# Autocorrelation of a two-layer decoder: the shifted sums as two products of 64 rows over mirrored tokens

## Chip, cores and metric

The kernel runs on one core of a Trainium2 chip. The metric is the device time of one execution in microseconds (us). The core has five engines with queues of their own: PE (TensorE, matrix products and transposes), DVE (VectorE), ACT (ScalarE), POOL (GpSimd) and SP (SyncE, which here only issues transfers). An engine takes its instructions in order; an instruction that waits holds up what is queued behind it on that engine.

## The reference, cut to what matters

A decoder of two layers over 8 samples of 128 tokens and 512 channels: block attention, autocorrelation with a context, and a mixture of experts in layer 0; attention over 256 tokens, cross attention and a second mixture in layer 1. The change is in the autocorrelation. In it Q is the sequence, K and V are both the context:

```
qf = jnp.fft.fft(q, axis=2)
kf = jnp.fft.fft(k, axis=2)
corr = jnp.fft.ifft(qf * jnp.conj(kf), axis=2).real
topk = int(C * np.log(L))                       # 9
w, idx = jax.lax.top_k(corr.transpose(0, 1, 3, 2), topk)
w = jax.nn.softmax(w, axis=-1)
pos = jnp.arange(L)[:, None]
for i in range(topk):
    g = jnp.minimum(idx[:, :, None, :, i] + pos, L - 1)
    out = out + w[:, :, None, :, i] * jnp.take_along_axis(v, g, axis=2)
```

Each channel picks nine shifts, and sums its context shifted by them, weighted; a shift past the last token reads the last token.

## The kernel before

A tile has the 128 tokens of a sample in the partitions and 512 channels along the row (or, after a transposition, 128 channels in the partitions and 4 x 128 tokens). All is float32; the profile shows every product of float32 as two passes on PE. The autocorrelation is done with matrices of cosines and sines, which lie in the table `dft` (its columns at T_A, T_I, T_W, T_V, T_J).

Samples go in four pairs, each an object of `Correlated`, in these steps:

- `spectra`: the waves of the sequence (pa) and of the context (pb), 64 frequencies each (L398); the two samples of a pair lie in the lower and upper 64 partitions. ACT copies pa out (xa), DVE multiplies (pr, L408 and L410), POOL adds and subtracts (L409, L411).
- `correlate`: the inverse transform, products of 64 rows (pc, L420), copied out by ACT (co, L425).
- `chosen(h)` for each sample: the nine largest shifts by MAX8 and match_replace on DVE (L435 to L441, into wk1, a tile of one buffer), exp of the differences (POOL L443, ACT L444), the mask (DVE L445), sum and reciprocal (L447, L449), and the normalized weights ex (POOL L450).
- `shifted(h)`: ex transposed (pt_wT, L129; copied out as wT), the waves of the context over 255 tokens (pvf, L460) and of the weights (pw, L464), each as two products of 128 rows, cosine and sine; ACT copies pw out twice (wf, L469 and L470), so that DVE can take it in the other order; DVE multiplies (vw, L472 and L474), POOL adds and subtracts (L473, L475).
- `done(h)`: back to tokens (poc), residual and layer norm (DVE L103, L91 to L95, POOL L97 for the root, DVE L107).

The context of a pair is loaded by `context(p)` (L314) into two buffers, tag "ct". For pairs 0 and 1 the steps stand as `pieces` in the loop of layer 0's attention (L516 to L547), two places a round: between its exps, its value products and its projections. `spectra` and `correlate` of pair 2 come behind that loop (L550 to L560); the rest of pair 2 and pair 3 stands in the mixture of experts, whose steps R (routing), E (experts) and T (tokens turned) are interleaved by hand with `chosen`, `shifted` and `done` (L731 to L768). In the following, samples are numbered 0 to 7, two to a pair. The order on every engine follows from the order of the calls, but for places under `issue_after`, which hold an instruction back behind a named one, and from which buffers are free.

Of the kernel before, what the change touches and what calls it, by code (L numbers as in the profile page):

```python
# [11 lines left out]
F32 = mybir.dt.float32  # L12
AF = mybir.ActivationFunctionType
ALU = mybir.AluOpType
# [3 lines left out]
P = 128  # L18
B, S, D = 8, 128, 512
NC = D // P  # L20
# [10 lines left out]

C_CAUSAL, C_HEAD = 0, 3 * P
C_SIGN = 3 * P + 2
N_MASK = 3 * P + 3
T_A, T_I, T_W, T_V, T_J = 0, P, 3 * P, 5 * P, 7 * P
N_DFT = 9 * P


def bc(ap, shape):
# [4 lines left out]
def decoder(ctx: ExitStack, tc: tile.TileContext, a: dict, out: bass.AP):  # L44
# [34 lines left out]
    causal = masks[:, C_CAUSAL : C_CAUSAL + 3 * P]  # L79
    pair = masks[:, C_HEAD : C_HEAD + 2]  # L80
    sign = masks[:, C_SIGN : C_SIGN + 1]

    def mm_acc(ps, pairs):
        n = len(pairs)
# [296 lines left out]
    def swapped(t):  # L381

        return t[:, 1:3, :]

    class Correlated:
# [5 lines left out]
        def spectra(self):  # L391

            ps = {}
            for n, src in (("a", xs), ("b", cts)):
                ps[n] = banks(f"p{n}_{self.p}")
                for i in range(2):
                    for h, b in enumerate(self.bs):
                        nc.tensor.matmul(  # L398
                            ps[n][64 * h : 64 * h + 64, i, :],
                            lhsT=dft[:, T_A + 64 * i : T_A + 64 * i + 64], rhs=src[b], start=True, stop=True,  # L400
                        )
                if n == "a":
                    xa = cp.tile([P, 3, D], F32, tag="sp", name=f"xa_{self.p}", bufs=2)
                    nc.scalar.copy(xa[:, 0:2, :], ps[n])

                    nc.scalar.mul(xa[:, 2, :], ps[n][:, 0, :], sign)
            self.pr = [cp.tile([P, 2, D], F32, tag="prod", name=f"pr_{self.p}_{i}", bufs=3) for i in range(2)]
            nc.vector.tensor_tensor(self.pr[0], ps["b"], xa[:, 0:2, :], ALU.mult)  # L408
            nc.gpsimd.tensor_tensor(self.pr[0][:, 0, :], self.pr[0][:, 0, :], self.pr[0][:, 1, :], ALU.add)  # L409
            nc.vector.tensor_tensor(self.pr[1], ps["b"], swapped(xa), ALU.mult)  # L410
            nc.gpsimd.tensor_tensor(self.pr[1][:, 0, :], self.pr[1][:, 0, :], self.pr[1][:, 1, :], ALU.subtract)  # L411

        def correlate(self):
            pc = banks(f"pc_{self.p}")
            for i in range(NC):
                cols = slice(i * P, (i + 1) * P)
                for n in range(2):
                    for h in range(2):
                        rows = slice(64 * h, 64 * h + 64)
                        nc.tensor.matmul(  # L420
                            pc[:, h, cols], lhsT=self.pr[n][rows, 0, cols],
                            rhs=dft[rows, T_I + n * P : T_I + (n + 1) * P], start=(n == 0), stop=(n == 1),
                        )
            self.co = cp.tile([P, 2, NC, P], F32, tag="co", name=f"co_{self.p}")
            nc.scalar.copy(self.co.rearrange("p h c t -> p h (c t)"), pc)  # L425

        def chosen(self, h):

            b, co = self.bs[h], self.co[:, h]

            top = sm.tile([P, NC, 8], F32, tag="top", name=f"top_{b}")
            nxt = sm.tile([P, NC, 8], F32, tag="nxt", name=f"nxt_{b}")
            wk1 = cp.tile([P, NC, P], F32, tag="wk1", name=f"wk1_{b}")
            for i in range(NC):
                nc.vector.max(top[:, i, :], co[:, i, :])  # L435
                nc.vector.match_replace(wk1[:, i, :], top[:, i, :], co[:, i, :], BIG)
                nc.vector.max(nxt[:, i, :], wk1[:, i, :])

            nc.vector.memset(nxt[:, :, TOPK - 8 :], BIG)
            for i in range(NC):  # L440
                nc.vector.match_replace(wk1[:, i, :], nxt[:, i, :], wk1[:, i, :], BIG)  # L441
            ex = cp.tile([P, NC, P], F32, tag="ex", name=f"ex_{b}", bufs=2)
            nc.gpsimd.tensor_tensor(ex, co, bc(top[:, :, 0:1], [P, NC, P]), ALU.subtract)  # L443
            nc.scalar.activation(ex, ex, AF.Exp)  # L444
            nc.vector.scalar_tensor_tensor(ex, wk1, BIG, ex, ALU.is_equal, ALU.mult)  # L445
            su = sm.tile([P, NC], F32, tag="su", name=f"su_{b}")
            nc.vector.tensor_reduce(su, ex, AX.X, ALU.add)  # L447
            rc = sm.tile([P, NC], F32, tag="rcw", name=f"rcw_{b}")
            nc.vector.reciprocal(rc, su)  # L449
            nc.gpsimd.tensor_tensor(ex, ex, bc(rc.unsqueeze(2), [P, NC, P]), ALU.mult)  # L450
            self.ex[h] = ex

        def shifted(self, h):
            b = self.bs[h]
            wT = cp.tile([P, NC, P], F32, tag="wT", name=f"wT_{b}")
            transposed(self.ex[h].rearrange("p c t -> p (c t)"), NC, P, wT, f"wT_{b}", "a")
            pv = banks(f"pvf_{b}")
            pw = banks(f"pw_{b}")
            for i in range(2):
                nc.tensor.matmul(  # L460
                    pv[:, i, :], lhsT=dft[:, T_V + i * P : T_V + (i + 1) * P], rhs=cts[b], start=True, stop=True
                )
            for i in range(2):
                nc.tensor.matmul(  # L464
                    pw[:, i, :], lhsT=dft[:, T_W + i * P : T_W + (i + 1) * P],
                    rhs=wT.rearrange("p c t -> p (c t)"), start=True, stop=True,
                )
            wf = cp.tile([P, 3, D], F32, tag="sp", name=f"wf_{b}", bufs=2)
            nc.scalar.copy(wf[:, 0:2, :], pw)  # L469
            nc.scalar.copy(wf[:, 2, :], pw[:, 0, :])  # L470
            vw = [cp.tile([P, 2, D], F32, tag="prod", name=f"vw_{b}_{i}", bufs=3) for i in range(2)]
            nc.vector.tensor_tensor(vw[0], pv, wf[:, 0:2, :], ALU.mult)  # L472
            nc.gpsimd.tensor_tensor(vw[0][:, 0, :], vw[0][:, 0, :], vw[0][:, 1, :], ALU.add)  # L473
            nc.vector.tensor_tensor(vw[1], pv, swapped(wf), ALU.mult)  # L474
            nc.gpsimd.tensor_tensor(vw[1][:, 0, :], vw[1][:, 1, :], vw[1][:, 0, :], ALU.subtract)  # L475
            self.ri[h] = [t[:, 0, :] for t in vw]

# [38 lines left out]
    for n, (p, f) in enumerate(steps):  # L516
        if f == 0:
            oTs.append(ap.tile([P, 2, NC, P], F32, tag="oT", name=f"oT0_{p}"))
        qT, kbd = qk
        units = []  # L520
        for j in range(2):
            toks = slice(j * P, (j + 1) * P)
            of = lambda i, w, p=p, f=f, j=j: vs[p, j][i].rearrange("p a x d -> p (a x d)")[:, f * w : (f + 1) * w]
            units.append((qT[:, toks], kbd[:, :, toks], lambda of=of: of(0, 192), lambda of=of: of(1, 128)))
        now = Heads16(ap, units, causal_bias, oTs[p][:, :, f, :], f"a0_{p}_{f}")
        now.exps(0)
        catch_up(now.scored)

        if turned:
            turned.out()  # L530
        if n + 1 < len(steps):
            qk = queries_keys(*steps[n + 1])
        if prev:
            prev.turn()
        auto(n, 0)

        for made in values_at.get(n, ()):
            values(*made)
        now.exps(1)
        if 0 < f < 3 and p:  # L540
            projection(2 * p - 3 + f, oTs[p - 1])
        if f == 1 and p and p + 1 < NP:
            xts.append(tokens(p + 1))
        auto(n, 1)
        if n >= begun and f == NC - 1:
            context(n // NC)
        turned, prev = prev, now  # L547
    assert not beside
# [4 lines left out]
    transposed(xs[1], NC, P, fp_tokens[1], "xTf0_1", "a")  # L553
    prev.turn()
    autos_of[2].spectra()
    prev.out()
    for j in range(2):
        projection(B - 2 + j, oTs[NP - 1])
# [184 lines left out]
    R(2)  # L743
    third.shifted(1)
    fourth.spectra()
    E(1)
    T(3)
    third.done(1)
# [519 lines left out]
def _mask_table():  # L1268
# [3 lines left out]
    t[:, C_CAUSAL : C_CAUSAL + 3 * P] = np.concatenate([half, half])  # L1272
    t[:, C_HEAD : C_HEAD + 2] = (np.arange(P)[:, None] // HD) % 2 == np.arange(2)
    t[:, C_SIGN] = np.where(np.arange(P) % 64 == 0, -1.0, 1.0)
    return t


# [11 lines left out]
def _dft_table():  # L1289
# [15 lines left out]
    for n, part in enumerate((cos, sin)):  # L1305
        t[:, T_I + n * P :][:, :P] = np.concatenate([2 * part / S] * 2)

    n = 2 * S - 1
    cos, sin = waves(n, np.arange(n), s)
    t[:, T_W : T_W + P], t[:, T_W + P : T_W + 2 * P] = cos[:S], sin[:S]  # L1310
    for i, whole in enumerate((cos, sin)):

        t[: S - 1, T_V + i * P :][:, :P] = whole[: S - 1]
        t[S - 1, T_V + i * P :][:P] = whole[S - 1 :].sum(0)
    c = np.where(s == 0, 1.0, 2.0)[:, None] / n
    cos, sin = waves(n, s, s)
    t[:, T_J : T_J + P], t[:, T_J + P : T_J + 2 * P] = c * cos, c * sin
    return t.astype(np.float32)


# [6 lines left out]
def _layouts(i):  # L1327
# [9 lines left out]
        "x": x,  # L1337
        "xT": xT,
        "ctx": c,
        "ctxT": cT,  # L1340
        "masks": _mask_table(),
        "dft": _dft_table(),
# [55 lines left out]
```

## Time and profile before

| | |
|---|---|
| three runs | 880.20, 883.38, 884.53 us, median 883.38 |
| profiled execution | 883.9 us; its span 882.1 us, so 1.8 us lie around the span |
| mean granted clock of PE | 0.994 |
| DVE, ACT, POOL busy | 62%, 42%, 21% of the span |
| transfers | 50.73 MB, 58 GB/s over the span |

On PE, from pa to the last poc, pair 0 lies at 85 to 146 us, pair 1 at 145 to 203, pair 2 at 208 to 259, pair 3 at 250 to 312. The transposed weights (pt_wT) and the products behind them come at 112 and 129 us for samples 0 and 1, at 174 and 191 for samples 2 and 3, at 231 and 245 for 4 and 5, at 274 and 292 for 6 and 7. A row of the timeline gives the start and the length of a run of like instructions in us, the engine, the line, the operation, the tiles (out<-in), the shapes, and in brackets how long the engine had been idle and what ended that. A row of the waits gives the engine and the line that waited, what for, the total in us, how often, and the longest. "Pass" below is one MATMUL record.

### The profile page before, as it was taken

To read this page: it belongs to the slowest core of one execution; us is meant where nothing else is said; L and a number is where in the kernel's file an instruction comes from. 1 tells how busy PE (TensorE), PEld (TensorE's weight loads), DVE (VectorE), ACT (ScalarE), POOL (GpSimd) and SP (SyncE) were. 2 spreads that over 40 slices of the span, in tenths; PEclk is the share of its full clock that TensorE was granted. 3 is DMA by queue.
4 is the path that set the end of the run, shared out by engine and by line. 5 is a ranking of instruction groups with operands and counts; after the bars stand their busy time and mean duration, and the time that the engine had idled before them with its cause. 6 is when DMAs were issued, how large, how long until landed. Compare 5 with 4: busy or idle time off the path is not lost.

```text
span 882.1 us, 17898 instructions
## 1 busy us (share of the span) xinstructions
PE 853.1 (97%) x6482; PEld 529.9 (60%) x6482; DVE 545.8 (62%) x2166; ACT 369.3 (42%) x1535; POOL 188.5 (21%) x267
## 2 busy tenths in 40 slices
PE   9999999999899999999999999999999999999996
PEld 5766655655455455555555687758475846576454
DVE  3656787777869567777778622735363545467654
ACT  3877564754222136666666503213122322224310
POOL 2500223133333314555555300000000000000000
PEclk9999999999999999999999999999999999999999
DMA  8700000130300002000004010331213211313340
GB/s 327 306 2 26 1 14 13 49 108 1 144 13 24 1 1 97 2 1 2 2 2 145 27 72 1 75 88 42 48 37 85 44 47 37 83 43 76 81 97 36
DMA packets 30073, 50.73 MB, mean 58 GB/s; under 512 B 5536, under 2 KB 22048, under 8 KB 28192
## 3 DMA queue, kind: packets, MB, share of 16 engines
q1 hardware_dynamic: 27424, 47.49, 17.9%
q10 hardware_dynamic: 2560, 2.10, 1.1%
q8 instruction: 51, 0.84, 0.4%
q14 instruction: 38, 0.31, 0.1%
HBM read 30.69 MB, written 2.10 MB: 37 GB/s over the span
## 4 chain that ended last, share of the span: by engine, by line
PE 72%; DVE 17%; ACT 6%; POOL 2%; issue 1%; DMA 1%; SPq 0%; ACTq 0%; POOLq 0%; DVEq 0%
PE pqx L86 9%; PE pox L994 7%; PE pv L86 5%; PE pkx L86 4%; PE pvx L86 4%; PE s_x L932 4%; PE o_x L977 4%; PE pq L86 4%; PE pk L86 3%; PE po L711 3%; ACT e_a L197 3%; DVE e_a L184 3%; PE pt_a L228 3%; PE pof L618 2%; PE s_a L165 2%; PE po L86 2%
## 5 line engine op out<-in xcount | busy, mean ns | idle before, releaser
L197 ACT ACTIVATE e_a<-e_a,m_a 128x128 f32<-128x128 f32 (+1 forms) x512 | 184.8, 365 | 100.2 <-DVE m_a L184 100.2
L953 ACT ACTIVATE e_x<-s_x,m_x 128x256 f32<-128x256 f32 x128 | 58.6, 483 | 140.0 <-DVE m_x L943 132.1
L197 ACT ACTIVATION_READ_ACCUMULATOR e_a<-e_a,m_a 128x1 f32 x512 | 97.6, 191 | 0.0
L86 PE MATMUL pqx<-xTx,w_X_q 128*128 128x256 f32 x384 | 84.9, 380 | 0.0
L86 PEld LDWEIGHTS pqx<-xTx,w_X_q 128*128 128x128 f32 x384 | 72.6, 190 | 11.4 <-issue 1.8
L994 PE MATMUL pox<-w_X_o,oTx 128*128 128x512 f32 x168 | 74.1, 596 | 0.7 <-DVE oTx L983 0.6
L942 DVE TENSOR_REDUCE m_x<-s_x 128x4 f32<-128x1024 f32 x32 | 37.6, 1218 | 41.2 <-PE s_x L932 41.2
L97 POOL TENSOR_TENSOR rs_x<-ve_x,neghalf 128x1 f32<-128x1 f32 x7 | 3.8, 548 | 268.8 <-DVE ve_x L95 249.8
L211 POOL TENSOR_TENSOR e_a<-e_a,rc_a 128x512 f32<-128x512 f32 (+1 forms) x64 | 52.7, 845 | 34.9 <-DVE rc_a L208 19.3
L994 PEld LDWEIGHTS pox<-w_X_o,oTx 128*128 128x128 f32 x168 | 31.3, 190 | 40.9 <-issue 39.2
L932 PE MATMUL s_x<-kTx,qTx 32*128 32x256 f32 x768 | 50.0, 385 | 1.2 <-ACT e_x L953 1.1
L228 PE MATMUL pt_a<-ident,e_a 128*128 128x128 f32 x384 | 48.0, 273 | 2.7 <-DVE m_a L184 2.7
L228 PEld LDWEIGHTS pt_a<-ident,e_a 128*128 128x128 f32 x384 | 43.6, 140 | 11.1 <-issue 5.0
L184 DVE CUSTOM_DVE_ANT_0 e_a<-s_a,masks 128x128 f32<-128x128 f32 (+1 forms) x256 | 47.1, 252 | 4.5 <-PE s_a L165 3.2
L932 PEld LDWEIGHTS s_x<-kTx,qTx 32*128 32x128 f32 x768 | 39.0, 184 | 17.4 <-issue 11.7
L184 DVE CUSTOM_DVE_ANT_0 e_a<-s_a,alibi 128x128 f32<-128x128 f32 (+1 forms) x256 | 47.4, 253 | 2.2 <-PE s_a L165 1.3
L977 PE MATMUL o_x<-pT_x,vx 128*32 128x512 f32 x384 | 43.7, 595 | 1.9 <-issue 0.7
L184 DVE DVE_READ_ACCUMULATOR2_ANT m_a<- 128x1 f32 x512 | 42.4, 83 | 0.1
L961 DVE STREAM_TRANSPOSE e_x<-e_x 128x1024 f32<-128x1024 f32 x32 | 39.7, 1241 | 0.8
L960 DVE TENSOR_SCALAR e_x<-e_x,rc_x 128x256 f32<-128x256 f32 x128 | 36.3, 347 | 3.9 <-DVE rc_x L957 2.2
L165 PEld LDWEIGHTS s_a<-kbd,qT 32*64 32x64 f32 x1024 | 20.7, 131 | 28.5 <-issue 15.4
L103 DVE TENSOR_TENSOR x_x<-pox,x_a 128x512 f32<-128x512 f32 x7 | 4.8, 686 | 52.5 <-PE pox L994 52.5
(236 smaller groups left out, 1627.1 us busy)
## 6 DMA issues: line engine op xcount, KB each, us to landing
pT_x<-e_x SPq DMA_DIRECT2D x224, 64.0 KB, 2.0
w_X_q<-in_X_q SPq DMA_DIRECT2D x3, 1024.0 KB, 4.8
w_X_o<-in_X_o SPq DMA_DIRECT2D x3, 1024.0 KB, 4.7
w_L_Wv<-in_L_Wv SPq DMA_DIRECT2D x2, 1024.0 KB, 7.3
w_L_Wo<-in_L_Wo SPq DMA_DIRECT2D x2, 1024.0 KB, 8.0
x_in<-in_x SPq DMA_DIRECT2D x8, 256.0 KB, 8.5
ct<-in_ctx SPq DMA_DIRECT2D x8, 256.0 KB, 2.6
cT<-in_ctxT SPq DMA_DIRECT2D x4, 512.0 KB, 3.8
```

The lines of the kernel that those rows point to most:

```text
L86: nc.tensor.matmul(ps, lhsT=l, rhs=r, start=(i == 0), stop=(i == n - 1))
L165: nc.tensor.matmul(s[r // 2][64 * u : 64 * u + 64, r % 2, cols], lhsT=qT[rows, 64 - 64 * part : P - 64 * part], rhs=kbd[rows, :, :keys], s ...
L184: self.scored = nc.vector.tensor_tensor_reduce(self.e[:, r, cols], s[i][:, r % 2, cols], bias(r, cols), -1.0, 3e38, ALU.add, ALU.min, self ...
L197: nc.scalar.activation(e[:, r, x, :], e[:, r, x, :], AF.Exp, scale=-1.0, bias=self.m[:, part, r, x : x + 1], accum_out=self.su[:, part, r, ...
L211: nc.gpsimd.tensor_tensor(e, e, bc(self.rc[:, part, rs, :].unsqueeze(3), list(e.shape)), ALU.mult)
L228: nc.tensor.transpose(pt[:, r, cols], self.e[:, 2 * i + r, cols], ident)
L932: nc.tensor.matmul(sc[g // 2][:, g % 2, u * 256 : (u + 1) * 256], lhsT=qT[rows, (h0 + u) * NS + n, :], rhs=kT[rows, n], start=(n == 0), st ...
L942: nc.vector.tensor_reduce(m, self.s[i], AX.X, ALU.max, negate=True)
L953: nc.scalar.activation(self.e[:, :, j, :], self.s[half][:, i, :].rearrange("p (a k) -> p a k", k=32), AF.Exp, bias=self.m[:, j : j + 1], s ...
L961: nc.vector.transpose(self.e[:, :, js, :], self.e[:, :, js, :])
L977: nc.tensor.matmul(po[32 * g : 32 * g + 32, :], lhsT=v[:, s, g * XD + 32 * n : g * XD + 32 * n + 32], rhs=pT[:, s].rearrange("p i h x -> p ...
L994: nc.tensor.matmul(po, lhsT=oT[:, n, h * P : (h + 1) * P], rhs=w, start=(i == 0), stop=(i == NX - 1))
```

## The change

Context and weights are split into sums and differences of mirrored tokens, so that cosine needs only the sums and sine only the differences: 64 rows each. The tables T_W and T_V shrink from 256 to 128 columns (cosine in rows 0 to 63, sine in rows 64 to 127), the table `dft` from 1152 to 896. What is new per pair and per sample:

- `spectra` also issues two transfers of 256 KB for each sample, the context in a mirrored order (`ctx_down`) and another order (`ctx_up`); the second takes a buffer of tag "ct".
- `folded`, called at the end of `correlate`: per sample one DVE scalar_tensor_tensor that makes sums and differences, held back behind `Correlated.behind` (the last MAX of the step's scores in the loop, the variance of the last layer norm in the later part), one transfer of the last token's row to 64 partitions, and two POOL subtracts on 64 partitions.
- `chosen`: two more POOL operations of 128x256 that add and subtract the weights' halves, one read backwards; they write into wk1, which is then what `shifted` transposes.
- `shifted`: pvf and pw are each two products of 64 rows, in the upper and the lower half of the rows; the second ACT copy (L470) goes, since DVE reads wf backwards.
- xa has one buffer instead of two; wf has a tag of its own, with one buffer.
- the call context(3) moves from the last round of the loop behind `spectra` of pair 2.

```diff
             nc.gpsimd.tensor_tensor(self.pr[1][:, 0, :], self.pr[1][:, 0, :], self.pr[1][:, 1, :], ALU.subtract)
+            self.folds = [cp.tile([P, D], F32, tag="ct", name=f"fold_{b}", bufs=2) for b in self.bs]
+            self.down = [cp.tile([P, D], F32, tag="down", name=f"down_{b}", bufs=2) for b in self.bs]
+            for b, f, down in zip(self.bs, self.folds, self.down):
+                nc.sync.dma_start(down, a["ctx_down"][b])
+                nc.sync.dma_start(f, a["ctx_up"][b])
+
+        def folded(self):
+            for b, f, down in zip(self.bs, self.folds, self.down):
+                with tc.issue_after(Correlated.behind.ins):
+                    nc.vector.scalar_tensor_tensor(f, down, fold, f, ALU.mult, ALU.add)
+                end = cp.tile([P, D], F32, tag="down", name=f"end_{b}", bufs=2)
+                nc.sync.dma_start(end[:64, :], a["ctx"][b, S - 1].partition_broadcast(64))
+                for _ in range(2):
+                    nc.gpsimd.tensor_tensor(f[:64, :], f[:64, :], end[:64, :], ALU.subtract)
+                cts[b] = f
...
             nc.scalar.copy(self.co.rearrange("p h c t -> p h (c t)"), pc)
+            self.folded()
...
             nc.gpsimd.tensor_tensor(ex, ex, bc(rc.unsqueeze(2), [P, NC, P]), ALU.mult)
-            self.ex[h] = ex
+            up, down = ex[:, :, 64:], ex[:, :, 63::-1]
+            for i, op in enumerate((ALU.add, ALU.subtract)):
+                nc.gpsimd.tensor_tensor(wk1[:, :, 64 * i : 64 * i + 64], up, down, op)
+            self.ex[h] = wk1
...
-            for i in range(2):
+            halves = [slice(64 * i, 64 * i + 64) for i in range(2)]
+            for i, rows in enumerate(halves):
+                nc.tensor.matmul(pv[:, i, :], lhsT=dft[rows, T_V : T_V + P], rhs=cts[b][rows], start=True, stop=True)
+            for i, rows in enumerate(halves):
                 nc.tensor.matmul(
-                    pv[:, i, :], lhsT=dft[:, T_V + i * P : T_V + (i + 1) * P], rhs=cts[b], start=True, stop=True
+                    pw[:, i, :], lhsT=dft[rows, T_W : T_W + P], rhs=wT[rows].rearrange("p c t -> p (c t)"),
+                    start=True, stop=True,
                 )
-            for i in range(2):
-                nc.tensor.matmul(
-                    pw[:, i, :], lhsT=dft[:, T_W + i * P : T_W + (i + 1) * P],
-                    rhs=wT.rearrange("p c t -> p (c t)"), start=True, stop=True,
-                )
-            wf = cp.tile([P, 3, D], F32, tag="sp", name=f"wf_{b}", bufs=2)
-            nc.scalar.copy(wf[:, 0:2, :], pw)
-            nc.scalar.copy(wf[:, 2, :], pw[:, 0, :])
+            wf = cp.tile([P, 2, D], F32, tag="wf", name=f"wf_{b}")
+            nc.scalar.copy(wf, pw)
...
-            nc.vector.tensor_tensor(vw[0], pv, wf[:, 0:2, :], ALU.mult)
+            nc.vector.tensor_tensor(vw[0], pv, wf, ALU.mult)
...
-            nc.vector.tensor_tensor(vw[1], pv, swapped(wf), ALU.mult)
+            nc.vector.tensor_tensor(vw[1], pv, wf[:, ::-1, :], ALU.mult)
...
         now.exps(0)
         catch_up(now.scored)
+        Correlated.behind = now.scored
...
-        if n >= begun and f == NC - 1:
+        if begun <= n < len(steps) - 1 and f == NC - 1:
             context(n // NC)
...
     autos_of[2].spectra()
+    context(3)
     prev.out()
...
     third.shifted(1)
     fourth.spectra()
+    Correlated.behind = moments.done
     E(1)
```

More of the change, by code (lines that the diff above doesn't have):

```diff
@@ L33 @@
 C_SIGN = 3 * P + 2
-N_MASK = 3 * P + 3
-T_A, T_I, T_W, T_V, T_J = 0, P, 3 * P, 5 * P, 7 * P
-N_DFT = 9 * P
+C_FOLD = 3 * P + 3
+N_MASK = 3 * P + 4
+T_A, T_I, T_W, T_V, T_J = 0, P, 3 * P, 4 * P, 5 * P
+N_DFT = 7 * P
 def bc(ap, shape):
@@ L81, in decoder @@
     sign = masks[:, C_SIGN : C_SIGN + 1]
+    fold = masks[:, C_FOLD : C_FOLD + 1]
     def mm_acc(ps, pairs):
@@ L402, in spectra @@
                 if n == "a":
-                    xa = cp.tile([P, 3, D], F32, tag="sp", name=f"xa_{self.p}", bufs=2)
+                    xa = cp.tile([P, 3, D], F32, tag="sp", name=f"xa_{self.p}")
                     nc.scalar.copy(xa[:, 0:2, :], ps[n])
@@ L1274, in _mask_table @@
     t[:, C_SIGN] = np.where(np.arange(P) % 64 == 0, -1.0, 1.0)
+    t[:, C_FOLD] = np.sign(63.5 - np.arange(P))
+    t[64, C_FOLD] = 0.0
     return t
@@ L1306, in _dft_table @@
         t[:, T_I + n * P :][:, :P] = np.concatenate([2 * part / S] * 2)
[L1308 to L1314, printed above, removed]
+    n, j = 2 * S - 1, np.arange(64)
+    t[:, T_W : T_W + P] = np.concatenate(waves(n, j + 0.5, s))
+    cos, sin = waves(n, j, s)
+    cos[0] = 0.5
+    sin[0] = s == 0
+    t[:, T_V : T_V + P] = np.concatenate([cos, sin])
     c = np.where(s == 0, 1.0, 2.0)[:, None] / n
-    cos, sin = waves(n, s, s)
+    cos, sin = waves(n, s, s + 0.5)
     t[:, T_J : T_J + P], t[:, T_J + P : T_J + 2 * P] = c * cos, c * sin
+    t[0, T_J + P :] = 1.0
     return t.astype(np.float32)
@@ L1339, in _layouts @@
         "ctx": c,
+        "ctx_up": c[:, np.r_[63:127, 127, 64:127]],
+        "ctx_down": c[:, np.r_[63:-1:-1, 127, 62:-1:-1]],
         "ctxT": cT,
```

## The prediction

> **What bounds the kernel now.** I read the page's busy table first, then the windows by stage, then what PE waits for between 80 and 320 us, where the autocorrelation lives, and last the timeline around each of its eight samples.
>
> ```profile
> span 882.1 us, 17898 instructions
> PE 853.1 (97%) x6482; PEld 529.9 (60%) x6482; DVE 545.8 (62%) x2166; ACT 369.3 (42%) x1535; POOL 188.5 (21%) x267
> ```
> ```profile
> core 0: us, PE busy (x) PEld busy (x) DVE busy (x) ACT busy (x) POOL busy (x), PEclk, DMA share, GB/s
> 110.00:140.00 30.00, 29.06 (x255) 17.65 (x254) 24.63 (x117) 18.78 (x78) 9.06 (x11) 1.00 0.07 20
> 215.00:250.00 35.00, 31.69 (x122) 17.02 (x122) 28.33 (x109) 8.27 (x18) 11.49 (x22) 0.95 0.26 98
> 280.00:320.00 40.00, 39.99 (x128) 20.94 (x127) 24.80 (x61) 7.46 (x18) 12.90 (x16) 1.00 0.03 13
> ```
> ```profile
> PE pvf L460 <- ACT wf L470: 2.0, 1, 2.0
> PE pt_wT L129 <- POOL ex L450: 1.3, 1, 1.3
> PE pw L464 <- ACT wT L139: 0.6, 1, 0.6
> PE s_a L165 <- DVE vw L474: 0.6, 2, 0.3
> ```
>
> PE is the bound (97%), but not everywhere. From 215 to 250 us it idles 3.3 of 35 us and is granted 0.95 of its clock; 280 to 320 it has no gap, so a delay earned before 280 is kept to the end. The waits name who ends PE's gaps around the changed code: POOL's normalized weights, ACT's copies, DVE's vw.
>
> **The saving on PE.** The next rows are PE's timeline: four passes of 128 rows, and the existing 64-wide products (pa, pb), which already run two beside each other.
>
> ```profile
> 86.64 1.89 PE L398 MATMUL pb<-ct,dft 128*64 128x512 f32 x8
> 88.45 1.55 PE L86 MATMUL pv<-w_L_Wv,xT 128*128 128x512 f32 x3
> ...
> 129.88 1.88 PE L460 MATMUL pvf<-ct,dft 128*128 128x512 f32 x4
> 131.59 1.88 PE L464 MATMUL pw<-wT,dft 128*128 128x512 f32 x4
> 133.31 3.60 PE L86 MATMUL po<-w_L_Wo,oT 128*128 128x512 f32 x8
> ```
>
> pvf and pw take 133.31 − 129.88 = 3.43 us a sample, 0.43 a pass. Eight pb passes take 88.45 − 86.64 = 1.81, that is 0.45 a pair. If the new 64-row products pair like that (as the 64*128 pc products do: 32 passes in about 2 us), eight passes cost four pairs, 1.8, and some 0.2 for entering and leaving the other shape: about 2.0, a saving of 1.45 us. Bounds: 0 where the two halves are not neighbours on PE, 1.7 with no edge cost. In the built order the pvf halves of samples 4, 5 and 6 are apart (pt_wT or gate products stand between), so these save only pw: 0.86 − 0.3, about 0.55.
>
> What it is worth by sample. Samples 1 and 3 (130 to 137, 191 to 198 us): PE has no gap, and what follows is PE work: −1.45 each, **−2.9**. Samples 0 and 2: what follows waits for DVE.
>
> ```profile
> 119.75 1.22 DVE L474 TENSOR_TENSOR vw<-pvf,wf 128x1024 f32<-128x1024 f32 x1
> 121.02 0.88 PE L165 MATMUL s_a<-kbd,qT 32*64 32x256 f32 x22 [0.28 <-DVE vw L474]
> ```
>
> vw stands in DVE's order behind sample 1's match, exp mask, su and rcw (113.8 to 118.7), which themselves wait for e_a's exps at 115.7; none gets earlier. PE's 0.28 gap becomes 0.28 + 1.45 = 1.73 (up to 2.4 if the additions below push DVE by the 0.6 of POOL's ex). Saving 0. The risk is the clock: after gaps of 1.98 (at 236.9) and 1.89 (at 359.3) the trace shows about 3.4 us at half clock, 1.7 us lost; after 1.33 (at 230.9) none. 1.73 lies between; I take half of 2 × 1.7, **+1.7** (bounds 0 and 3.4). The Trainium skill, "TensorE: Matmul & The Clock Gate", Part 1, says that the gate judges free-running windows of about 3.4 us, so whether such a gap throttles depends on its phase; by that a gap of 1.7 may cost nothing, and the sum would be 1.7 lower. Sample 7 (292 to 296): PE-bound, pairs intact, **−1.2** (0.8 to 1.45).
>
> **Fold and end, pairs 0 and 1.** Added per pair: two 256 KB loads per sample (the row of the same kind, ct from in_ctx, lands in 2.6 us), one DVE scalar_tensor_tensor each (nearest row L445, 128x512, 0.69), a 128 KB broadcast each (small loads land in 2.0 to 2.3), two POOL subtracts each. A two-input POOL row at 128x512 is 1.27 (L409); 64 partitions are not cheaper (copies of 64x256 and of 128x256 both take 0.40), so 1.27 each, 5.1 a pair; lower bound half of it. DVE idles 1.19 at 95.4, POOL idles 99.6 to 104.0; the four subtracts push ex (L443, 103.98) by some 0.6, and the two weight operations, 0.65 each (L211 at 128x256 takes 0.651; no row has a reversed operand, so 0.40, the copy, to 1.27), end near 111.4, before pt_wT at 112.12. Cost 0; cover gone, about 1 a pair. The dropped ACT copies (L470, 0.59 a sample) free nothing that PE waits for here.
>
> **Pair 2.** POOL's and DVE's timelines:
>
> ```profile
> 218.83 1.89 DVE L107 TENSOR_SCALAR x_a<-x_a,mv_a,rs_a 128x512 f32<-128x512 f32 x1 [0.66 <-POOL rs_a L97]
> 222.53 0.55 POOL L97 TENSOR_TENSOR rs_a<-ve_a,neghalf 128x1 f32<-128x1 f32 x1 [2.09 <-DVE ve_a L95]
> 229.85 1.04 POOL L450 TENSOR_TENSOR ex<-ex,rcw 128x512 f32<-128x512 f32 x1 [3.31 <-DVE rcg L607]
> 230.91 0.27 DVE L436 MATCH_REPLACE8 wk<-top,co 128x128 f32<-128x128 f32 x1
> 230.94 0.66 PE L129 MATMUL pt_wT<-ident,ex 128*128 128x128 f32 x4 [1.33 <-POOL ex L450]
> 236.89 2.06 PE L460 MATMUL pvf<-ct,dft 128*128 128x512 f32 x2 [1.98 <-ACT wf L470]
> ```
>
> The loads reuse ct's buffers, so they wait for pb (211.9) and land at 214.6; the folds run to 216.1 in a gap of DVE; the end rows land near 217.7. In the built order POOL takes subtract, rs_a_6, subtract, subtract, subtract, ten memsets (1.7), rs_a_7: 217.7 + 4 × 1.27 + 0.55 + 1.7 = 225.0, where rs_a_7 started at 222.53: +2.5. DVE's L107 waits for it, and sample 4's top, match and all of chosen stand behind L107. Then two weight operations, 1.3, before pt_wT: 230.94 + 2.5 + 1.3 = 234.7. Next, the weights now lie in wk1, which has one buffer: sample 5's first match_replace (230.91) waits until pt_wT has read it, 235.3. Its match, mask and vw (4 to 4.5 us, with 2.4 for the products) follow, so vw's POOL adds end near 244.0 against 240.3, and poc, 241.27 before, starts there; pg (1.8) and pt_wT_5 come at 247.4 against 244.7: +2.7, less 0.55 for pw of sample 5. About +2.1. PE's gap before 234.7 is over 4 us, so half clock is likely on pt_wT and pw of sample 4, +1.3; before's own throttle at 236.9 may go. I take **+3.0**, bounds +1 and +5.
>
> The row at 218.83 is a DVE tensor_scalar of 0.55 (at 223.11) held to 1.89 while POOL runs memsets; L608 goes 0.21 to 1.06 beside L450. The Trainium skill, "SBUF — State Buffer", Who interferes with whom, adds that a DVE operation with two SBUF inputs contends with a POOL operation that reads SBUF, the later one blocked for the whole of the other. That speaks against the folds, which have two SBUF inputs: by it they would wait for pr's subtract (214.52 to 215.78) and the sum would be about 1 higher; no row shows L445 beside POOL, and my sum leaves it out.
>
> **Pair 3.**
>
> ```profile
> 253.64 1.23 DVE L408 TENSOR_TENSOR pr<-pb,xa 128x1024 f32<-128x1024 f32 x1 [2.20 <-PE pb L398]
> 259.86 1.27 POOL L411 TENSOR_TENSOR pr<-pr 128x512 f32<-128x512 f32 x1 [3.65 <-DVE pr L410]
> 262.58 0.55 POOL L97 TENSOR_TENSOR rs_c<-ve_c,neghalf 128x1 f32<-128x1 f32 x1 [0.94 <-DVE ve_c L95]
> 264.11 0.29 DVE L435 MAX8 top<-co 128x8 f32<-128x128 f32 x1 [0.40 <-ACT co L425]
> ```
>
> The loads wait for pb (253.5), land at 256.2; the folds stand directly behind L408 on DVE, so x_f (257.19), st_f and L410 behind them slip 0.45. End rows land at 259.2; POOL: two subtracts (261.8), pr's subtract (263.1 instead of 261.1, so pc's second half +2), subtract, rs_f, subtract, rs_c at 266.1 instead of 262.58. DVE's L107 of x_c blocks sample 6's first MAX8: 267.3 against 264.11, +3.2. Then rs_f (0.55, now ahead) and two weight operations (1.3): pt_wT of sample 6, at 273.75 with no slack, +5.0; pw gives 0.55 back, and PE's own gaps there (0.34 and 0.61) absorb some. I take **+4.0**, bounds +2 and +6. The moved context(3) and the 24 extra SP issues (0.33 each) stand ahead of alibi, Wv and lnv, wanted no sooner than 296: cost 0; uncovered, 2.6.
>
> **Sum**: −2.9 + 1.7 − 1.2 + 3.0 + 4.0 = +4.6 on the profiled 883.9 (span 882.1 and 1.8 around it), 888.5. That execution stands 0.5 above the median of 883.38, so the forecast is **888.0**.
>
> **Rivals.**
> - *No net change* (880 to 887): no throttle in samples 0 and 2, pairs 2 and 3 at the middle of their lower halves (+2, +3): −2.9 − 1.2 + 5 = +0.9, 884.3. For it: 3.3 us of idle in 215 to 250 which a delay could refill. Against: that idle comes before the place where wk1 and poc bind.
> - *The saving reaches the end*: POOL's subtracts run at half my price (0.64, as if partitions or overlap counted), so rs_a and rs_c are no later, and only the 1.3 of weights remains in each pair, mostly absorbed: −2.9 − 1.2 + 0.8 = −3.3, 880.1; with samples 0 and 2 paying half, 878.7. It decides when four subtracts end before 221.8 and rs_c before 263. For it: POOL is busy in 21% of the span and its gaps are wide. Against: 64x256 copies cost as much as 128x256.
> - *Worse by the shared path*: a folded STT or a reversed operand on POOL is slower, each DVE tensor_scalar meets a POOL operation (L107 + 1.3, as at 218.83, twice a pair): +4.6 + 2 × 2 × 1.3 = +9.8, with half clocks in every gap, 893.2 to 895. For it: rows 218.83 and L608. Against: most L107 rows in these stretches are 0.55.
> - *It doesn't do what it says*: the halves don't run beside each other, saving 0: +4.6 + 2.9 + 1.2 + 1.1 − 1.7 (no new gaps) = +8.1, 891.5. Against: pb and pc.
>
> **How the numbers follow.** What a measurement here can tell from no change is about 0.5%, 4.4 us: below 879.0 is faster, above 887.8 slower. Forecast 0.47 (885 to 892), no net change 0.21, saving reaches the end 0.13, worse 0.13, not paired 0.06. Slower: 0.30 of the forecast's mass and all of the last two, 0.49. Faster: nearly all of the third and a trace of the others, 0.12. The same: 0.39. The range, 880 to 895, leaves out most of the third case and little of the fourth.
>
> **What would show it.** Right: pt_wT of sample 4 near 234.7 (plus or minus the shift so far) with POOL as releaser; L436 of sample 5 waiting for PE pt_wT; rs_c near 266; pvf and pw together 2.0 us at samples 0 to 3 and 7; PE's gap before s_a 1.7 at samples 0 and 2. Wrong: subtracts near 0.64, a PE clock of 1.00 from 215 to 250, or pvf passes still 0.43 apart.

## The result, and the profile after

The changed kernel takes 894.86 us (median of 6 runs, 889.98 to 897.89) against 881.33 us (6 runs, 880.20 to 884.53): a ratio of 1.0144, 95% interval 1.0108 to 1.0179, so 13 us slower. Its profiled execution took 897.89 us, with a span of 896.1; it is the slowest of the six, whose times go with their mean granted clock (889.98 us at 0.991, 897.89 at 0.981).

The head of the page of the changed kernel:

```profile
span 896.1 us, 17977 instructions
PE 855.7 (95%) x6482; PEld 529.1 (59%) x6482; DVE 552.8 (62%) x2174; ACT 365.9 (41%) x1527; POOL 219.9 (25%) x299
```

PE is busy for as long as before although its work became smaller, POOL has 31 us more to do, and 14 us of span were added. The windows by stage (us; busy time and count of each engine, granted clock of PE, DMA share, GB/s):

```profile
110.00:140.00 30.00, 27.20 (x251) 16.56 (x252) 24.47 (x117) 17.75 (x75) 12.40 (x15) 0.94 0.08 19
180.00:215.00 35.00, 32.42 (x371) 19.74 (x370) 26.03 (x101) 19.42 (x77) 11.00 (x14) 0.95 0.20 68
215.00:250.00 35.00, 27.92 (x95) 14.46 (x94) 24.32 (x91) 5.24 (x11) 16.93 (x26) 0.78 0.34 122
280.00:320.00 40.00, 37.61 (x117) 18.45 (x116) 30.61 (x105) 8.32 (x17) 15.67 (x19) 0.96 0.05 14
...
234.50:251.50 17.00, 13.54 (x25) 6.01 (x26) 11.99 (x45) 3.21 (x6) 6.80 (x8) 0.50 0.06 15
```

The third number from the end, PE's clock, is the news: 1.00 has become 0.94 and 0.95 in the stages of samples 0 and 2, and 0.95 has become 0.78 in pair 2, where PE ran 17 us without a break at half clock although it was busy for 13.5 of them. What PE waited for between 80 and 330 us (total, times, longest):

```profile
PE pt_wT L131 <- DVE gx L632: 7.1, 1, 7.1
PE s_a L167 <- DVE vw L496: 3.6, 2, 1.8
PE pc L440 <- POOL pr L413: 2.8, 1, 2.8
PE pg L88 <- ACT xTf L141: 2.3, 1, 2.3
```

All four are new or grown. The first is put down to DVE's gx, which came last in the profile's reckoning; in POOL's timeline below the weight sum that pt_wT reads ends at 237.91, 0.05 before PE starts, so POOL is taken as the releaser. First PE at sample 1, where the saving was expected, and at sample 0, where a gap was:

```profile
121.56 1.37 PE L167 MATMUL s_a<-kbd,qT 32*64 32x256 f32 x22 [1.79 <-DVE vw L496]
...
132.07 1.13 PE L485 MATMUL pvf<-fold,dft 64*128 64x512 f32 x4
133.03 1.02 PE L487 MATMUL pw<-wT,dft 64*128 64x512 f32 x4
133.99 3.70 PE L88 MATMUL po<-w_L_Wo,oT 128*128 128x512 f32 x8
```

pvf and pw now take 133.99 − 132.07 = 1.92 us instead of 3.43: the halves do run beside each other. In sample 0 PE waits 1.79 us, and from 121.8 to 125.2 it is at half clock. Pair 2 on DVE, POOL and PE:

```profile
215.94 2.17 DVE L426 SCALAR_TENSOR_TENSOR fold<-down,masks,fold 128x512 f32<-128x512 f32 x2 [0.16 <-issue]
218.02 0.68 DVE L105 TENSOR_TENSOR x_a<-po,x_in 128x512 f32<-128x512 f32 x1
...
215.63 1.26 POOL L413 TENSOR_TENSOR pr<-pr 128x512 f32<-128x512 f32 x1
220.49 1.26 POOL L430 TENSOR_TENSOR fold<-fold,end 64x512 f32<-64x512 f32 x1 [3.60 <-DMA end<-in_ctx]
221.71 0.54 POOL L99 TENSOR_TENSOR rs_a<-ve_a,neghalf 128x1 f32<-128x1 f32 x1
222.23 4.02 POOL L430 TENSOR_TENSOR fold<-fold,end 64x512 f32<-64x512 f32 x3
227.85 0.55 POOL L99 TENSOR_TENSOR rs_a<-ve_a,neghalf 128x1 f32<-128x1 f32 x1
237.19 0.72 POOL L474 TENSOR_TENSOR wk<-ex 128x256 f32<-128x256 f32 x1
...
237.96 1.12 PE L131 MATMUL pt_wT<-ident,wk 128*128 128x128 f32 x4 [7.08 <-DVE gx L632]
239.19 0.09 DVE L457 MATCH_VALUE_LOAD wk<-top,co 128x8 f32 x1 [1.24 <-PE pt_wT L131]
```

The second rs_a, 222.53 before, stands behind four subtracts and the memsets at 227.85, and PE waits 7.08 us. The last row is sample 5's first match: it waited 1.24 us for pt_wT to read wk1, as predicted. Pair 3 on DVE and POOL has the same picture, with pr's subtract and rs_c (259.86 and 262.58 before) behind the subtracts:

```profile
265.67 1.42 DVE L426 SCALAR_TENSOR_TENSOR fold<-down,masks,fold 128x512 f32<-128x512 f32 x2 [1.54 <-DMA fold<-in_ctx_up]
269.43 2.60 POOL L430 TENSOR_TENSOR fold<-fold,end 64x512 f32<-64x512 f32 x2 [3.94 <-DMA end<-in_ctx]
271.99 1.26 POOL L413 TENSOR_TENSOR pr<-pr 128x512 f32<-128x512 f32 x1
276.85 0.56 POOL L99 TENSOR_TENSOR rs_c<-ve_c,neghalf 128x1 f32<-128x1 f32 x1 [0.64 <-DVE ve_c L97]
```

To see where the time goes, the same PE instructions are compared in both traces: start in a run's trace less start in the trace of before. The growth of this shift between two places is what the stage between them cost in us. Each row is one profiled execution: that of the kernel before lies 2.6 above the median given with the result, that of the changed kernel 3.0 above its own, e5's 4.3, the others within 1.9. The last column is the time at half clock between 80 and 330 us, 3.4 before.

| run | until pa of pair 0 | samples 0 to 3 | pair 2 (to pa of pair 3) | pair 3 (to pt_wT of sample 7) | sample 7 (to pq) | half clock |
|---|---|---|---|---|---|---|
| changed kernel | +0.5 | +0.5 | +7.6 | +6.2 | −1.4 | 27.3 |
| e1 weights only | +0.6 | −1.1 | −1.4 | +1.5 | −0.6 | 3.4 |
| e2 context only | +0.5 | −0.9 | +5.1 | +4.0 | −0.5 | 13.7 |
| e3 pvf twice | +1.1 | −2.6 | +3.7 | +7.3 | −1.4 | 13.7 |
| e4 not beside | +0.4 | 0.0 | +4.8 | +6.1 | 0.0 | 10.2 |
| e5 end on DVE | +0.6 | +0.3 | +4.5 | +3.4 | −1.4 | 23.9 |
| e6 sums first | +0.6 | −1.1 | −2.3 | +1.0 | −0.6 | 0 |
| e8 all | +0.3 | −2.8 | −1.0 | +1.2 | −1.4 | 3.4 |
| e9 pvf first | −0.1 | −0.6 | +1.7 | +2.6 | −3.4 | 6.8 |
| e10 subtract later | +0.9 | +3.4 | +1.1 | +4.4 | −1.4 | 20.5 |
| e11 later in 2, 3 | −0.1 | −1.0 | +5.0 | +5.1 | −1.4 | 23.9 |
| e12 context in 0, 1 | +0.7 | −2.8 | −2.3 | +1.0 | −0.6 | 0 |

The first column is the start of the kernel, which varies by about 1 us between the traces; of the change only the width of `dft` lies in it. In e9 pvf of sample 7 stands ahead of pt_wT and two passes of pq ahead of pw, so its last two stages can't be set beside those of the others.

### The profile page after: what moved, and what is told of

Read it like the earlier page. It is cut to its first block, busy times and chain, and to the rows that moved or that the text cites. A ratio compares the mean times of both kernels' runs of the same rounds, so it can differ in the third digit from the quotient of the medians.

```text
span 896.1 us, 17977 instructions
## 1 busy us (share of the span) xinstructions
PE 855.7 (95%) x6482; PEld 529.1 (59%) x6482; DVE 552.8 (62%) x2174; ACT 365.9 (41%) x1527; POOL 219.9 (25%) x299
## 4 chain that ended last, share of the span: by engine, by line
PE 66%; DVE 17%; ACT 6%; POOL 4%; DMA 2%; issue 1%; SPq 1%; ACTq 1%; POOLq 0%; DVEq 0%
PE pqx L88 9%; PE pox L1019 7%; PE pv L88 5%; PE pvx L88 4%; PE s_x L957 4%; PE o_x L1002 4%; PE pq L88 3%; PE pkx L88 3%; PE pk L88 3%; PE po L735 3%; ACT e_a L199 3%; DVE e_a L186 3%; PE pt_a L230 3%; PE s_a L167 2%; PE po L88 2%; PE pof L642 2%
## 5 line engine op out<-in xcount | busy, mean ns | idle before, releaser
L167 PE MATMUL s_a<-kbd,qT 32*64 32x256 f32 (+1 forms) x1024 | 34.3, 341 | 5.1 <-DVE vw L496 3.6
```

Of the source, the lines that this page charges most:

```text
L167: nc.tensor.matmul(s[r // 2][64 * u : 64 * u + 64, r % 2, cols], lhsT=qT[rows, 64 - 64 * part : P - 64 * part], rhs=kbd[rows, :, :keys], s ...
```

## The experiments

Ratios are against runs of the kernel before on the same chips. Theory A: the folds' subtracts stand ahead of the layer norms' roots in POOL's queue, and PE's gaps that follow bring half clock on top. Its rivals are the weight sums with the one buffer wk1 (C), the shorter work of PE itself (B), and the folds' loads and DVE work (D).

**e1, weights only.**

```diff
-            self.folded()
-                nc.tensor.matmul(pv[:, i, :], lhsT=dft[rows, T_V : T_V + P], rhs=cts[b][rows], start=True, stop=True)
+                nc.tensor.matmul(pv[:, i, :], lhsT=dft[:, T_V + i * P : T_V + (i + 1) * P], rhs=cts[b], start=True, stop=True)
-    cos, sin = waves(n, s, s + 0.5)
+    cos, sin = waves(n, s, s + 63.5)
```

> Only the weights are split into sums and differences; the context is used as before (no loads of mirrored context, no folds, no subtracts; pvf is two products of 128 rows). Theory A (the folds' subtracts stand ahead of the layer norms' roots on POOL, and the stall that follows puts PE at half clock): rs_a of sample 7 and rs_c are on time again, what stays is 1.4 us of weight sums ahead of pt_wT in pairs 2 and 3 and the wait for wk1, some +1 to +3 a pair, against -0.7 each in samples 1, 3 and 7: 880 to 886 us, no half clock of over 4 us around 235. Rival C (the weight sums and the one buffer wk1 make the loss): 889 us or more, with PE's long gap before pt_wT of sample 4 still there.

Measured: 881.5 us, ratio 0.9984 (0.9971 to 0.9996). Half of the change costs nothing and gains a little; C falls as the main cause. What the weight sums cost is still to be seen in PE's waits of this run, 1.3 before:

```profile
PE pt_wT L131 <- POOL wk L468: 4.4, 2, 2.6
PE s_a L167 <- DVE vw L492: 1.5, 2, 0.7
```

With only pw shortened, s_a waits 0.7 each, and the stages of samples 0 and 2 keep full clock.

**e2, context only.**

```diff
-            for i, op in enumerate((ALU.add, ALU.subtract)):
-                nc.gpsimd.tensor_tensor(wk1[:, :, 64 * i : 64 * i + 64], up, down, op)
-            self.ex[h] = wk1
+            self.ex[h] = ex
```

> Only the context is folded; the weights go unsplit through two products of 128 rows, as before. Theory A: the subtracts still hold rs_a (about +4 us) and rs_c (about +5), the long gap before pt_wT of sample 4 and the half clock behind it stay: 887 to 893 us. Rival C: 880 to 884 us.

Measured: 891.4 us, 1.0096 (1.0081 to 1.0111). The time is as A said; rs_a of sample 7 starts at 226.31, 4.2 us late once the shift before pair 2 (−0.4) is taken off. The context half alone thus costs 0.96%, and the weights half alone nothing. The two together come to 0.8%, against 1.44% for the changed kernel: the rest appears only with both. By the table it lies in samples 0 to 3 (+0.5 against −1.1 − 0.9; only both cuts together make the gap of 1.79) and in pair 2 (7.6 against 5.1 − 1.4, with 17.1 us of half clock there against 10.2 in e2).

**e3, pvf made twice in samples 0 and 2.**

```diff
+            for _ in range(2 if h == 0 and self.p < 2 else 1):
                 for i, rows in enumerate(halves):
```

> The changed kernel, with the products pvf of samples 0 and 2 made twice (the same result), about 1 us more work for PE in front of each of its two gaps before s_a. If PE's idle 1.8 us is what brings the half clock there: both stretches (121.8 to 125.2 and 183.2 to 186.7) run at full clock and the kernel gets faster by 2 to 3.5 us, 891 to 893. If the half clock has another cause or PE's work counts there: no change or up to 2 us slower, 895 to 897.

Measured: 890.51 us, 1.0093 (1.0071 to 1.0114), 4.4 us less than the changed kernel by the medians. Its windows have full clock in the stages of both samples, the first two lines, and PE's gaps there are 0.9:

```profile
110.00:140.00 30.00, 27.62 (x261) 16.67 (x261) 25.94 (x132) 19.20 (x82) 12.83 (x15) 1.00 0.07 20
180.00:215.00 35.00, 33.27 (x377) 19.79 (x376) 27.54 (x102) 19.18 (x77) 12.90 (x15) 1.00 0.22 77
215.00:250.00 35.00, 27.54 (x110) 14.80 (x108) 26.29 (x102) 5.91 (x13) 18.63 (x29) 0.90 0.30 113
```

Useless work on PE makes the kernel faster: in these stages the idle gap costs, by the clock that it brings. The two profiled executions lie 6.4 us apart, and the table shows 3.1 of that in samples 0 to 3. Pair 2 is 3.9 cheaper in this trace with the same work and pt_wT of sample 4 as late as in the changed kernel (6.0 us and 5.9); its half clock lasted 6.8 us instead of 17.1.

**e4, nothing beside each other.**

```diff
-                nc.tensor.matmul(pv[:, i, :], lhsT=dft[rows, T_V : T_V + P], rhs=cts[b][rows], start=True, stop=True)
+                nc.tensor.matmul(pv[:, i, :], lhsT=dft[:, T_V + i * P : T_V + (i + 1) * P], rhs=cts[b], start=True, stop=True)
...
+        t[64 * i : 64 * i + 64, T_V + i * P : T_V + (i + 1) * P] = part
```

(pw and T_W likewise.)

> The changed kernel, its products pvf and pw made of 128 rows with tables padded with zeros, so that nothing runs beside each other; all else stays. Theory A: samples 0 and 2 lose their gap and half clock (-3.2 us), samples 1, 3 and 7 lose the saving (+1.45 each, +4.3), pairs 2 and 3 keep their stalls: 894 to 898 us. Rival B (the loss comes from PE having less to do, so that the clock falls): 881 to 885 us. If the halves had never run beside each other: no change anywhere.

Measured: 895.11 us, 1.0144 (1.0127 to 1.0161), the changed kernel's own ratio. B falls: with PE's work as long as before, pairs 2 and 3 still lose 4.8 and 6.1. What pairing gains in samples 1, 3 and 7 (1.4, 1.2 and 1.4) the half clock after samples 0 and 2 takes back for the most part (1.6 each).

**e5, the last token taken off on DVE.**

```diff
-                for _ in range(2):
-                    nc.gpsimd.tensor_tensor(f[:64, :], f[:64, :], end[:64, :], ALU.subtract)
+                    nc.vector.scalar_tensor_tensor(f[:64, :], end[:64, :], -2.0, f[:64, :], ALU.mult, ALU.add)
```

> The changed kernel, but the last token is taken off the folded context by one DVE operation (end * -2 + f) instead of two POOL subtracts; its transfer goes out with the other loads into a buffer of its own, and wf shares xa's buffer to make room. POOL's order of before the change comes back, but for the weight sums; DVE gets four operations of some 0.6 to 0.75 us a pair behind L408 or oT instead of two. Theory A (POOL's queue is what delays rs_a and rs_c): rs_a of sample 7 within +1.5 us and rs_c within +2 us of their place before, PE's gap before pt_wT of sample 4 falls from 7.1 to 3 us or less, the half clock around 235 to one or two stretches of 3.4 us, and the time to 883 to 888. Rival D (the folds cost through their loads and through DVE's order, whoever subtracts): 890 to 895.

Measured: 887.24 us, 1.0059 (1.0032 to 1.0085). rs_a of sample 7 is 1.2 us late instead of 4.2, rs_c 1.6 instead of 5.6 (each less the shift before its pair), PE's longest wait for pt_wT 4.0 instead of 7.1. The half clock missed the expectation: 13.7 us from 234.6 on. The nine runs spread from 882.5 us (mean clock 0.995) to 892.4 (0.983), and the profiled one, 891.5, is among the longest. D is right in part, the folds on DVE still cost something, and the weight sums stand undiminished.

**e6, the sums ahead of the normalization** (on top of e1).

```diff
+            up, down = ex[:, :, 64:], ex[:, :, 63::-1]
+            for i, op in enumerate((ALU.add, ALU.subtract)):
+                nc.gpsimd.tensor_tensor(wk1[:, :, 64 * i : 64 * i + 64], up, down, op)
             nc.vector.tensor_reduce(su, ex, AX.X, ALU.add)
...
-            nc.gpsimd.tensor_tensor(ex, ex, bc(rc.unsqueeze(2), [P, NC, P]), ALU.mult)
+            nc.gpsimd.tensor_tensor(ex, wk1, bc(rc.unsqueeze(2), [P, NC, P]), ALU.mult)
+            self.ex[h] = ex
```

> The kernel with only the weights split, and the two sums made on POOL from the masked weights while DVE still adds them up, and the normalization afterwards from wk1 into ex, which is transposed; the same arithmetic in another order. If the weight sums cost by standing in the chain between rcw and pt_wT: 0.9 us a sample comes off the gaps before pt_wT of samples 4 and 6 (2.6 and 1.8 us), wk1 is free earlier, and the time falls from 881.5 to 878 to 881. If not, no change.

Measured: 879.9 us, 0.997 (0.9959 to 0.9981). POOL's sums now run while DVE reduces:

```profile
228.19 1.41 POOL L463 TENSOR_TENSOR wk<-ex 128x256 f32<-128x256 f32 x2 [2.21 <-DVE ex L460]
229.68 1.04 POOL L468 TENSOR_TENSOR ex<-wk,rcw 128x512 f32<-128x512 f32 x1
```

PE's waits for pt_wT fall from 4.4 to 1.7 in all, and no half clock is left before 330 us.

**e8, both splits with the three remedies** (e5, e6's order, e3's repeated pvf). The three diffs are those shown at e5, e6 and e3.

> Both splits, the last token taken off on DVE, the sums ahead of the normalization, and pvf made twice in samples 0 and 2 to keep PE's clock. If the three costs add up as told (subtracts on POOL, sums in the chain, half clock behind the gaps), what is left are 1.45 us saved in samples 1, 3 and 7 and a loss of 1 to 3 us in pairs 2 and 3: 878 to 883 us. If the folds cost through DVE and the loads: 886 or more.

Measured: 879.95 us, 0.9973 (0.9959 to 0.9987), from the changed kernel's 1.0144: with the three remedies together the loss is gone. Each alone gives 0.85% (e5), 0.5% (e3) and 0.14% (e6 against e1).

**e9, pvf ahead of the transposition**, and twice in sample 4 too.

```diff
+            for _ in range(2 if h == 0 and self.p < 3 else 1):
+                for i, rows in enumerate(halves):
+                    nc.tensor.matmul(pv[:, i, :], lhsT=dft[rows, T_V : T_V + P], rhs=cts[b][rows], start=True, stop=True)
             wT = cp.tile([P, NC, P], F32, tag="wT", name=f"wT_{b}")
```

> The kernel of e8 with pvf asked for ahead of the transposition of the weights, so that its two halves stand beside each other in samples 4 and 5 too and run while PE waits for the weights; pvf is made twice in sample 4 as well. If PE's gap before pt_wT of sample 4 (2.7 us) is what brings the half clock at 230, and the lone halves cost: no half clock around 230 (-1.6 us) and some -0.9 each in samples 4 and 5, so 876 to 879 us against 880 of e8. If not, 879 to 881.

Measured: 885.33 us, 1.0019 (1.001 to 1.0028): a miss. PE at sample 4:

```profile
227.96 1.99 PE L480 MATMUL pvf<-fold,dft 64*128 64x512 f32 x8
232.26 0.66 PE L131 MATMUL pt_wT<-ident,ex 128*128 128x128 f32 x4 [2.32 <-POOL ex L470]
233.99 1.09 PE L131 MATMUL pt_xTf<-ident,x_c 128*128 128x128 f32 x4 [0.85 <-DVE hs L631]
236.56 2.08 PE L484 MATMUL pw<-wT,dft 64*128 64x512 f32 x4 [1.48 <-ACT wT L141]
```

The pvf half that had stood between pt_wT and pw covered ACT's copy of wT. Moved ahead, it leaves waits of 0.85 and 1.48 behind, besides 2.32 in front, and half clock for 6.8 us. More work ahead of a gap did not keep the clock here. Samples 0 to 3 lose as well, −0.6 instead of e8's −2.8: at sample 1 pvf and pw, now apart, take 2.12 us instead of 1.91, and the 32 passes of s_a behind them 1.66 instead of 0.84, at full clock. Why s_a slowed down is not shown.

**e10, the subtracts held back** behind each sample's ex, nothing replaced.

```diff
+            apart = nc.gpsimd.tensor_tensor(ex, co, bc(top[:, :, 0:1], [P, NC, P]), ALU.subtract)
+                with tc.issue_after(apart.ins):
+                    nc.gpsimd.tensor_tensor(f[:64, :], f[:64, :], end[:64, :], ALU.subtract)
```

> The changed kernel with nothing left out and nothing replaced; the POOL subtracts are only held back behind each sample's ex (top minus co), where POOL waits 2 to 3 us anyway, so that rs_a of sample 7, pr's second part and rs_c no longer stand behind them. If their place in POOL's queue makes the loss: rs_a of sample 7 and rs_c within 1.5 us of their place before, PE's gap before pt_wT of sample 4 from 7.1 to 4 us or less, 885 to 890 us. If the amount of POOL work makes it, wherever it stands: 892 to 897.

Measured: 892.54 us, 1.0103 (1.0085 to 1.0121). The time lies where the rival said; the stages don't. rs_a of sample 7 and rs_c are 0.6 and 0.8 us late, and pair 2 costs 1.1 instead of 7.6. But in samples 0 and 2 the subtracts delay ex and so vw: PE waits 2.5 us each for vw, and those stages cost 3.4. DVE shows another price of POOL's new place, a short operation of 0.2 us that ran 1.26 beside the subtracts:

```profile
231.40 2.60 POOL L469 TENSOR_TENSOR fold<-fold,end 64x512 f32<-64x512 f32 x2
231.44 1.26 DVE L629 TENSOR_SCALAR gx<-lg,topg 128x28 f32<-128x28 f32 x1
```

**e11, held back in pairs 2 and 3 only.**

```diff
+            if self.p >= 2:
+                with tc.issue_after(apart.ins):
+                    self.less(self.folds[h], self.ends[h])
```

> As e10, but the subtracts are held back in pairs 2 and 3 only; pairs 0 and 1 are as in the changed kernel, so samples 0 and 2 keep its gaps of 1.8 us and its half clock instead of e10's 2.5 us. By the place of the subtracts in POOL's queue: pair 2 (shift of pa of pair 3 less shift of pa of pair 2) costs 1 to 3 us instead of 7.6, pair 3 up to 4 instead of 6, together 886 to 890 us. If e10's shorter pair 2 was an accident of the clock: 892 to 897.

Measured: 889.17 us, 1.0062 (1.005 to 1.0075), inside the expected time, but pair 2 cost 5.0 and pair 3 5.1, more than expected. rs_a and rs_c are 0.6 and 1.0 late, as in e10, and pt_wT of sample 4 is 3.3 late in both (5.9 in the changed kernel); what follows differs by the clock, 13.7 us at half clock against 6.8. In sample 0 this trace has the changed kernel's gap, and no half clock behind it:

```profile
120.96 0.88 PE L167 MATMUL s_a<-kbd,qT 32*64 32x256 f32 x22 [1.79 <-DVE vw L505]
```

The traces say why. Within each of them the starts of half clock lie whole multiples of 3.413 us apart, and so mark the edges of windows of that length. In the changed kernel the gap of sample 0 (119.77 to 121.56) lies whole in the window that ends at 121.81. In e11 such a point, 120.50, falls into the gap and leaves 1.33 us in one window and 0.46 in the next.

**e12, the context folded in pairs 0 and 1 only**, weights as in e6.

```diff
-            self.folded()
+            if self.p < 2:
+                self.folded()
...
+            for i in range(2 if self.p >= 2 else 0):
+                nc.tensor.matmul(
+                    pv[:, i, :], lhsT=dft[:, T_V2 + i * P : T_V2 + (i + 1) * P], rhs=cts[b], start=True, stop=True
+                )
```

> The weights split in all samples with the sums ahead of the normalization, the context folded in pairs 0 and 1 only (subtracts on POOL, pvf twice in samples 0 and 2), pairs 2 and 3 as in e6. If the parts are worth what the stages of e6 and e8 showed (samples 0 to 3: -2.6 us in e8 against -0.6 in e6; pairs 2 and 3: -1.8 in e6 against -1.1 in e8): 877.5 to 879 us, faster than e6 and e8 by 1 to 2. If not: 879.5 to 881.

Measured: 877.86 us, 0.9937 (0.9922 to 0.9952), 0.6% faster than the kernel before. Each stage costs what its part cost alone: −2.8 in samples 0 to 3 as in e8, −2.3 and +1.0 in pairs 2 and 3 as in e6. Its window of pair 2 has full clock:

```profile
215.00:250.00 35.00, 31.26 (x132) 15.49 (x131) 28.71 (x110) 8.89 (x18) 15.98 (x27) 1.00 0.25 98
```

## Why the prediction came out as it did

The side was right, but the size was not: +13.5 by the medians where +4.6 was forecast. The time lies outside the forecast's own 885 to 892; the stated range, 880 to 895, reaches it by 0.14 us, thanks to a rival, which is luck. Pairs 2 and 3 both cost more than the upper bounds given for them. By steps:

- The saving on PE: 1.92 us for pvf and pw (about 2.0 forecast), worth 1.4, 1.2 and 1.4 in samples 1, 3 and 7 (−1.45, −1.45 and −1.2). e4 shows that it comes from the halves beside each other. The rival "it doesn't do what it says" falls.
- Samples 0 and 2: nothing saved, as argued, and a gap of 1.79 (1.73 forecast). "I take half of 2 × 1.7" was mis-sized: both gaps threw the clock, 1.6 us each. e3 shows the cause. In e11's trace the same 1.79 in sample 0 left the clock alone, because it fell across the edge of a window (see e11), so the outcome depends on the phase, as the prediction had said; half was a fair weight, and the profiled execution got the worse draw.
- Pairs 0 and 1, folds at no cost: right in the changed kernel; e12 saves 2.8 there with the folds in place.
- Pair 2, "I take +3.0, bounds +1 and +5": the failed step, 7.6. Two terms of it. First, the delay of pt_wT: 5.9 instead of 3.8. The folds, which the sum let run to 216.1 in DVE's gap at 0.69 each, took 2.17 together, beginning beside POOL's pr (215.63 to 216.89); in pair 0 they take 0.75 each, and in pair 3, away from POOL, two took 1.42. The end rows then took 3.0 us from issue to use instead of 2.3. That is 1.7; the weight sums at 0.72 with lnq between them add 0.4. The sum had left the wait of the folds out and named it as "about 1 higher". The Trainium skill, "SBUF — State Buffer", Who interferes with whom, has it that a DVE operation with two SBUF inputs and a POOL operation that reads SBUF block each other; this trace agrees, with 2.17 for two against 1.5.
- Second, the clock in pair 2: "half clock is likely on pt_wT and pw of sample 4, +1.3" allowed for one stretch, and the trace has five, 17.1 us. The same chain with 6.8 us of it (e3) cost 3.7, so the long stretch is worth 3.9. The two terms, 2.1 and 3.9, come to more than the 4.6 that was missing: what else the sum had for pair 2 was at least 1.4 too much, and the runs don't say which part.
- Pair 3, "+4.0, bounds +2 and +6": 6.2. The chain was as told, with rs_c at 268.2 on before's clock (266.1 forecast) and pt_wT of sample 6 7.0 late (+5.0). The subtracts began 1.5 later than forecast (260.7 on before's clock for 259.2): DVE's folds waited for loads that landed 0.8 later than forecast (256.97 for 256.2), and the end rows again took 3.0 us.
- The wait for wk1's one buffer (1.24 us in pair 2) and the sums behind rcw: e6 shortens both together and lies some 1.2 us below e1 by the two ratios, whose intervals overlap; they weren't taken apart.
- The rival "no net change" falls: PE's 3.3 idle us from 215 to 250 were not refilled, they became 7.1.
- The rival "worse by the shared path" named part of what happened (the folds held beside POOL, half clock behind the gaps), at 893 to 895, and came nearest on the time. Its price did not come out: it had two tensor_scalar rows a pair 1.3 longer, but of these rows (L109) in pairs 2 and 3 one alone grew, x_f's from 0.55 to 1.48, and x_a's first fell from 1.89 to 1.49. So its number is in part luck. "The saving reaches the end" turned on POOL's price for 64 partitions: the subtract takes 1.26, the full price, and it falls.

What stays open: why the half clock in pair 2 lasted 17.1, 13.7, 10.2 or 6.8 us, with 17.1 and 6.8 behind the same gap of 7.1 (the changed kernel and e3). In the changed kernel three of the five windows had gaps of at most 0.1 us in them and were still followed by another at half clock. No run varied this alone.

## What to carry to other kernels

Halving PE's work pays only where PE sets the end, and it can cost where the next instruction waits for another engine: the gap that it opens may halve PE's clock for a while. Before moving sums and folds to an idle engine, ask what stands behind them in that engine's queue: here 1.3 us of POOL work each did little harm in two pairs and cost several us in the other two, where 0.55 us roots of layer norms waited behind it. A scaling that commutes with a sum belongs behind it, if the sum can then run beside the reduction that the scaling waits for.

## What the runs showed of the hardware that was not expected

- PE idle for 1.79 us was followed by half clock in the changed kernel (twice) and not in e11's sample 0; 0.9 us in samples 0 and 2 of e3, e8 and e12 was never followed by it.
- The outcome goes with PE's idle time within one window of 3.413 us, by the rows of the profile. In all thirteen traces, from 80 to 860 us, each of the 32 windows at full clock with 1.78 us or more of it was followed by one at half clock, 4 of the 9 with 1.44 to 1.72, and none of the 2874 with 1.42 or less. The Trainium skill, "TensorE: Matmul & The Clock Gate", Part 1, says that the gate's window of about 3.4 us is free-running; the starts at whole multiples of 3.413 us and the two outcomes of one gap agree with it. The page has the slow state come after at least one idle window of about 3.4 us; here 1.78 us within one was enough, and the measurement decides.
- Between 80 and 860 us half clock came in multiples of 3.41 us (up to five), and went on while PE was busy for 13.5 of 17 us.
- A POOL subtract of two tiles takes 1.26 us on 64 partitions as on 128 (1.27); with one operand read backwards 128x256 took 0.72 against 0.65 forwards.
